# Attention in three sweeps, with each projection as seven products of 2x2 blocks over two token tiles

## The chip, the cores and the metric

One core of one Trainium2 chip runs the whole program. The time is device microseconds of one execution; the number given for a kernel is the median of its runs. The engines are named as the profile names them: PE does matmuls and PE transposes, PEld is its weight load, DVE and ACT are the vector and the scalar engine, POOL is the third one, and SP issues nearly all DMAs here. Everything is float32.

## The reference

The program is one pre-norm transformer block on 2048 tokens of width 1024. Attention runs inside a token: its 32 heads attend to each other, so that scores are a 32 x 32 matrix for each token. The MLP's three matrices (hidden width 2752) are quantized to 16 NF4 codes in blocks of 64 and restored before they are used.

```python
def attn(hidden_states, wq, bq, wk, bk, wv, bv, ...):        # H, D = 32, 32
    q = (hidden_states @ wq.T + bq).reshape(B, S, H, D)
    k = (hidden_states @ wk.T + bk).reshape(B, S, H, D)
    v = (hidden_states @ wv.T + bv).reshape(B, S, H, D)
    scores = jnp.einsum('bshd,bstd->bsht', q, k) / np.sqrt(D)
    probs = jax.nn.softmax(scores, axis=-1)
    return jnp.einsum('bsht,bstd->bshd', probs, v).reshape(B, S, E)

def nf4_quant_dequant(w):                                    # BLOCKSIZE = 64
    flat = w.reshape(-1, BLOCKSIZE)
    absmax = jnp.max(jnp.abs(flat), axis=1, keepdims=True)
    normalized = flat / jnp.where(absmax == 0, 1.0, absmax)
    bounds = (NF4_CODE[:-1] + NF4_CODE[1:]) * 0.5
    return (NF4_CODE[jnp.searchsorted(bounds, normalized)] * absmax).reshape(shape)

def ffn(x, w1, w2, w3):
    gate = jnp.einsum('bsd,hd->bsh', x, nf4_quant_dequant(w1))
    up = jnp.einsum('bsd,hd->bsh', x, nf4_quant_dequant(w2))
    return jnp.einsum('bsh,dh->bsd', jax.nn.silu(gate) * up, nf4_quant_dequant(w3))

x = x + attn(layernorm(x), ...)
x = x + ffn(layernorm(x), w1, w2, w3)
```

## The kernel before

**Attention.** The loop over 16 tiles of 128 tokens (`for i in range(NT)`) keeps all of wq, wk and wv in SBUF (12 MB). A tile is normed (`normed`, DVE and POOL), transposed by PE into `xnT` (and, with its tokens in another order, `xnV`), and projected: `project` at L317 does eight accumulating matmuls of 128 x 128 by 128 x 512 for each half of the output, 48 in all. DVE transposes each half out of PSUM in 32 x 32 blocks (`qk_half` L328, `v_half` L335) and adds the bias. Scores and contexts of the tile before are 32 x 32 matmuls, 128 for each call of `scores` (L345) or `context` (L379), two calls for a tile. Softmax (L359), the residual sum (L398) and the second layer norm are mostly DVE's. `keep_T` (L410) transposes the normed tile for the MLP and stores it, with the four operand differences that the MLP's products need, in DRAM.

**The MLP** works on two halves of 1024 tokens (`tbp`) and on groups of four 128-wide hidden chunks (`GROUPS`: 0 to 3, 4 to 7, ... 20 and 21, the last chunk half wide). A `Unit` (L622) computes gate and up of one chunk for one half, which are a 2x2 block product, by seven products of four matmuls instead of eight. `down` (L697) then multiplies a group's hidden values by its w3 chunks and adds them to the rows in DRAM. The order of the passes is group 0 half 0, group 0 half 1, group 1 half 1, group 1 half 0, and so on. Chunk 0 of half 0 is done plainly (`plain_block`, L557) while the attention of the last tile ends.

**The background.** The generator `background` (L196) restores the MLP's weights, one job of 128 x 1024 values at a time. A job's order is: for each chunk of a group ("1", c) and ("2", c), then ("3", c) for each chunk; 65 jobs in all, twelve for a full group. A job is 15 threshold passes, each an ACT instruction (`sg`, L211) and a DVE instruction (`r`, L214 for the first and L216 for the others), the block maxima and the scaling of the next job's input after the tenth pass (`absmax`, L177; `scaled`, L169: 16 short ACT instructions), and the scaling of its result. Every `yield` of the generator is called a step here: one at the very start and then 17 for each job (16 for the last). `advance(n)` (L228) issues n steps. A finished job is put into `pending`. What is left of it is done by `flush` (L164), which runs the generator `finish` (L134): a first call transposes half of the chunk on PE and copies it, a second does the other half, and a third stores it and enters its key into `wd`. The tile `r` of a job has two buffers, `sg` two, `wn` three and `wop` one.

**What sets the order.** PE's instructions run in the order in which the program writes them (`tc.manual_schedule`, L246). The orders of DVE, ACT and SP are chosen by a planner, from the order of the program, the dependences and the free buffers. Attention calls `advance` with 4, 3, 4, 4 and 3 in each tile. In the MLP `spent` (L534) is called with each product's nominal microseconds (3.43 for a product of four matmuls, 1.7 for each full chunk in each of the eight steps of `down`), issues RATE steps for each of them, and calls `flush(1)` when the running job is past its fifth pass. Whoever needs a restored weight calls `until` (L232) first: `load_w12` (L514) for each unit, `load_w3` (L524) for each chunk of a `down`.

```python
    def until(kind, c):                       # L232
        while (kind, c) not in wd:
            if next(bg, flush) is flush:      # flush is what next returns when bg is at its end
                flush()
```
```python
        if step["n"] in range(5, 15):         # L539, in spent
            flush(1)
        advance(n)
```

Of the kernel before, what the change touches and what calls it, by code (L numbers as in the profile page):

```python
# [12 lines left out]
FP = mybir.dt.float32  # L13
AF = mybir.ActivationFunctionType
ALU = mybir.AluOpType
# [18 lines left out]
RATE = 0.6  # L34
# [17 lines left out]
def preln_block_kernel(  # L52
# [184 lines left out]

    left, right = ExitStack(), ExitStack()
# [3 lines left out]
    ps_pj = left.enter_context(tc.tile_pool(name="ps_pj", bufs=4, space=PSUM, side="left"))  # L242
    work = right.enter_context(tc.tile_pool(name="work", bufs=1, side="right"))
# [4 lines left out]
    hook["pool"] = ps_pj  # L248

    def bank(nm):  # L250
        return hook["pool"].tile([P, TB], FP, tag="pj", name=nm)

    hook["psum"] = lambda half: bank("ptw").rearrange("p (k h) -> p k h", h=P)
    xt = {}

    def load_x(i):
        xt[i] = work.tile([P, E], FP, tag="x", name="xt")
        nc.sync.dma_start(xt[i], xf[ts(i, P), :])

    load_x(0)  # L260
    ws = []
    for nm, w in (("wq", wqT), ("wk", wkT), ("wv", wvT)):
        t = wpool.tile([P, KC, E], FP, tag=nm, name=nm)
        for n in range(2 if nm == "wq" else 1):
            m = 512 if nm == "wq" else E
            for k in range(KC):
                nc.sync.dma_start(t[:, k, ts(n, m)], w[ts(k, P), ts(n, m)])
        ws.append(t)
    biases = []
    for nm, b in (("qb", qb), ("kb", kb), ("vb", vb)):  # L270
        t = wpool.tile([P, 32], FP, tag=nm, name=nm)
        for g in range(4):
            nc.scalar.dma_start(t[g * 32 : (g + 1) * 32, :], b)
        biases.append(t)
    qb_sb, kb_sb, vb_sb = biases
    wq_sb, wk_sb, wv_sb = ws
# [9 lines left out]
    def normed_x(i):  # L286
        return normed(xt.pop(i), work.tile([P, E], FP, tag="xn", name="xn"))

    def transposed(xn, put):

        for half in range(2):
            pt = bank("pt").rearrange("p (k t) -> p k t", t=P)
            for k in range(4):
                nc.tensor.transpose(pt[:, k, :], xn[:, ts(4 * half + k, P)], ident)
            put(half, pt)

    def inputs_T(xn):
        xnT = work.tile([P, KC, P], FP, tag="xnT", name="xnT")

        xnV = work.tile([P, KC, P], FP, tag="xnV", name="xnV")  # L300
        pts = []

        def put(half, pt):
            nc.scalar.copy(xnT[:, ts(half, 4), :], pt)
            pts.append(pt)

        def put_v():
            for half, pt in enumerate(pts):
                nc.scalar.copy(
                    xnV[:, ts(half, 4), :].rearrange("p k (c m) -> p k c m", c=4),  # L310
                    pt.rearrange("p k (m c) -> p k c m", c=4),
                )

        transposed(xn, put)
        return xnT, xnV, put_v

    def project(lhsT, w, n, by_d=False):  # L317

        pj = bank("pj")
        for k in range(KC):  # L320
            rhs, dst = w[:, k, ts(n, 512)], pj
            if by_d:
                rhs = w[:, k, :].rearrange("p (t d) -> p t d", d=D)[:, :, ts(n, 16)]
                dst = pj.rearrange("p (t d) -> p t d", d=16)
            nc.tensor.matmul(dst, lhsT[:, k, :], rhs, start=(k == 0), stop=(k == KC - 1))  # L325
        return pj

    def qk_half(t, pj, n):  # L328

        nc.vector.transpose(  # L330
            t.rearrange("p s h -> p h s")[:, ts(n, 16), :],
            pj.rearrange("p (h d) -> p h d", d=D),
        )

    def v_half(t, pj, n):  # L335

        nc.vector.transpose(
            t.rearrange("p m d -> p d m")[:, ts(n, 16), :],
            pj.rearrange("p (t d) -> p d t", d=16),
        )  # L340

# [16 lines left out]

    def softmax_T(at):  # L359
# [15 lines left out]
        prT = work.tile([P, 32, NH], FP, tag="prT", name="prT")  # L375
# [3 lines left out]
    def context(at, prT, vd, part):  # L379
        for s4 in range(4 * part, 4 * part + 4):  # L380
            for g in range(4):
                m = 8 * g + s4
                for c in range(4):
                    r = slice(c * 32, (c + 1) * 32)
                    nc.tensor.matmul(
                        at[g * 32 : (g + 1) * 32, c, s4 * 32 : (s4 + 1) * 32],
                        prT[r, m, :],
                        vd[r, m, :],
                        start=True,
                        stop=True,  # L390
                    )

    def load_x1(i):
        x1 = work.tile([P, E], FP, tag="x1", name="x1")
        nc.sync.dma_start(x1, xf[ts(i, P), :])
        return x1

    def residual(i, at, x1):  # L398

        cx = work.tile([P, 32, NH], FP, tag="pr", name="cx").rearrange("p a b -> p (a b)")  # L400
# [7 lines left out]

    even = {}

    def keep_T(i, x1n):

        t = work.tile([P, 2, 4, P], FP, tag=f"xT{i % 2}", name="xT")
        transposed(x1n, lambda half, pt: nc.scalar.copy(t[:, half], pt))
# [16 lines left out]

    xnT, xnV, put_v = inputs_T(normed_x(0))
    put_v()
    prev = x1n = None
    for i in range(NT):
        if i + 1 < NT:
            load_x(i + 1)
# [367 lines left out]
```

## Time and profile before

| | us |
|---|---|
| median of 3 runs (2578.46 to 2581.49) | 2580.28 |
| the profiled execution | 2583.84 |
| its span | 2582.1 |
| PE busy in the span | 2503.7 (97%) |
| DVE busy | 1895.3 (73%) |
| ACT busy | 1804.1 (70%) |
| DMA traffic | 402 MB, 156 GB/s |

A group line of the profile names the line of the kernel, the engine and the operation, then output and inputs by tile name with their shapes, and how often it ran; behind the first bar stand its busy time and the mean of one in ns, behind the second the engine's idle time just before such instructions and what ended it. A matmul on 128 x 512 float32 values leaves two records. In a timeline a line is a run of like instructions: start, length, engine, line, operation, and in brackets the idle time before it and its releaser. A table by stage gives busy microseconds of each engine in a stretch of the span, with the number of instructions, the clock granted to PE, the busy share of the DMA engines and their GB/s. Attention lasts until about 843 us, where the first matmul of `plain_block` starts; the first unit begins at about 883, and the twelve calls of `down` start at 966, 1125, 1281, 1440, 1599, 1757, 1914, 2076, 2234, 2391, 2485 and 2546.

### The profile page before, as it was taken

How to read it: one execution, taken by the hardware profiler on the slowest of the kernel's cores; microseconds unless marked ns; L12 is line 12 of the kernel's file. 1: busy time of each engine (PE TensorE's matmuls, PEld its weight loads, DVE VectorE, ACT ScalarE, POOL GpSimd, SP SyncE). 2: the span in 40 equal slices, each digit the busy share in tenths (PEclk: the TensorE clock that was granted, in tenths of full speed). 3: DMA queues.
4: the chain of work that ended last, by engine and by line, in shares of the span. 5: the costliest groups of instructions: out<-in, count | busy, mean ns of one | idle time of the engine just before them, and what ended most of it. 6: DMA issues, size and time to landing. Idle time of an engine off the chain costs nothing.

```text
span 2582.1 us, 36864 instructions
## 1 busy us (share of the span) xinstructions
PE 2503.7 (97%) x14336; PEld 1168.0 (45%) x14336; DVE 1895.3 (73%) x2089; ACT 1804.1 (70%) x3494; POOL 26.5 (1%) x87
## 2 busy tenths in 40 slices
PE   8889999999998899999999999999999999999998
PEld 3445555555554444444444444444444444444433
DVE  4888888888887587787888788777887887751222
ACT  3866565665655597998989898898998998851000
POOL 0000000000000000000000000000000000000000
PEclk9899999999999899999999999999999999999999
DMA  7022222312222866344663346544464354551483
GB/s 261 18 99 97 70 83 91 99 59 91 71 77 89 301 235 235 117 147 175 248 220 142 140 171 248 204 147 155 163 252 171 136 198 160 211 203 66 150 293 138
DMA packets 135167, 402.21 MB, mean 156 GB/s; under 512 B 11664, under 2 KB 65936, under 8 KB 120272
## 3 DMA queue, kind: packets, MB, share of 16 engines
q1 hardware_dynamic: 134416, 399.81, 43.2%
q8 instruction: 112, 1.84, 0.3%
q14 instruction: 63, 0.52, 0.1%
q10 hardware_dynamic: 576, 0.05, 0.0%
HBM read 268.48 MB, written 131.33 MB: 155 GB/s over the span
## 4 chain that ended last, share of the span: by engine, by line
PE 25%; ACT 20%; DVE 17%; issue 6%; DMA 2%; DVEq 0%; SPq 0%; ACTq 0%
DVE r L216 14%; PE po L714 10%; PE z L548 8%; ACT sg L211 8%; ACT r L172 5%; ACT wn L172 4%; PE q L548 3%; PE rr L548 2%; ACT wop L147 1%; DVE am L184 1%; DMA w<-wd 1%; DVE acc L735 1%; PE po L726 1%; PE ptw L146 1%; ACT u L647 0%
## 5 line engine op out<-in xcount | busy, mean ns | idle before, releaser
L211 ACT ACTIVATE sg<-wn,edge 128x1024 f32<-128x1024 f32 (+1 forms) x975 | 1097.6, 1139 | 264.5 <-DVE r L216 241.5
L216 DVE SCALAR_TENSOR_TENSOR r<-sg,r 128x1024 f32<-128x1024 f32 (+1 forms) x910 | 1103.9, 1213 | 122.5 <-ACT sg L211 72.2
L714 PE MATMUL po<-w,h 128*128 128x512 f32 x1344 | 597.5, 599 | 13.8 <-DVE acc L735 10.4
L714 PEld LDWEIGHTS po<-w,h 128*128 128x128 f32 x1344 | 250.7, 191 | 338.8 <-issue 288.6
L548 PE MATMUL z<-xB,w 128*128 128x512 f32 x720 | 322.0, 597 | 2.4 <-DVE h L685 1.4
L548 PE MATMUL z<-xT,w 128*128 128x512 f32 x656 | 297.2, 596 | 3.8 <-ACT g L640 2.9
L548 PE MATMUL q<-xT,w 128*128 128x512 f32 x656 | 291.5, 592 | 0.0
L172 ACT ACTIVATE wn<-wn,rc 128x64 f32<-128x64 f32 x1032 | 267.7, 336 | 26.8 <-DVE rc L192 26.7
L172 ACT ACTIVATE r<-r,am 128x64 f32<-128x64 f32 x1032 | 257.3, 336 | 14.4 <-DVE r L216 14.1
L325 PE MATMUL pj<-wv,xnV 128*128 128x512 f32 x512 | 230.6, 604 | 0.0
L325 PE MATMUL pj<-wq,xnT 128*128 128x512 f32 x512 | 230.1, 603 | 0.0
L325 PE MATMUL pj<-wk,xnT 128*128 128x512 f32 x512 | 227.9, 598 | 0.0
L735 DVE TENSOR_TENSOR acc<-acc,po 128x512 f32<-128x512 f32 x192 | 129.9, 682 | 132.8 <-PE po L714 87.3
L548 PEld LDWEIGHTS z<-xB,w 128*128 128x128 f32 x720 | 135.7, 192 | 167.6 <-issue 158.5
L548 PEld LDWEIGHTS z<-xT,w 128*128 128x128 f32 x656 | 122.9, 191 | 152.5 <-issue 139.3
L548 PEld LDWEIGHTS q<-xT,w 128*128 128x128 f32 x656 | 123.1, 190 | 148.1 <-issue 145.2
L184 DVE TENSOR_REDUCE am<-wn 128x16 f32<-128x1024 f32 (+1 forms) x65 | 78.6, 1209 | 144.7 <-ACT r L172 142.6
L147 ACT COPY wop<-ptw 128x512 f32<-128x512 f32 (+1 forms) x130 | 74.4, 573 | 128.4 <-PE ptw L146 128.4
L325 PEld LDWEIGHTS pj<-wv,xnV 128*128 128x128 f32 x512 | 97.5, 193 | 118.0 <-issue 117.1
L548 PE MATMUL rr<-xB,w 128*128 128x512 f32 x328 | 147.5, 592 | 0.0
L325 PEld LDWEIGHTS pj<-wq,xnT 128*128 128x128 f32 x512 | 96.4, 193 | 111.3 <-issue 107.0
L325 PEld LDWEIGHTS pj<-wk,xnT 128*128 128x128 f32 x512 | 94.8, 190 | 109.3 <-issue 108.1
(74 smaller groups left out, 1396.9 us busy)
## 6 DMA issues: line engine op xcount, KB each, us to landing
w<-wd SPq DMA_DIRECT2D x41, 1280.0 KB, 6.9
acc<-x1d SPq DMA_DIRECT2D x96, 512.0 KB, 3.9
wd<-wop SPq DMA_DIRECT2D x21, 2048.0 KB, 7.2
w<-wd SPq DMA_DIRECT2D x83, 512.0 KB, 4.8
x1d<-acc SPq DMA_DIRECT2D x80, 512.0 KB, 2.9
wn<-in_w_dram SPq DMA_DIRECT2D x63, 512.0 KB, 3.8
xT<-xdT SPq DMA_DIRECT2D x28, 1024.0 KB, 7.5
xB<-xdB SPq DMA_DIRECT2D x24, 1024.0 KB, 6.4
```

Source lines behind the costliest of these rows:

```text
L146: nc.tensor.transpose(pt[:q, k, :], v[:, j * q : (j + 1) * q], ident)
L147: nc.scalar.copy(o[:q, first + half], pt[:q])
L172: nc.scalar.mul(dst[:, ts(n, BLOCK)], src[:, ts(n, BLOCK)], by[:, n : n + 1])
L184: nc.vector.tensor_reduce(am[:, :nb], v.rearrange("p (b e) -> p b e", e=BLOCK), AX.X, ALU.max, apply_absolute_value=True,)
L211: nc.scalar.activation(t, v, AF.Identity, bias=edge[:, i : i + 1], scale=BIG)
L216: nc.vector.scalar_tensor_tensor(r, t, code, r, ALU.min, ALU.max)
L325: nc.tensor.matmul(dst, lhsT[:, k, :], rhs, start=(k == 0), stop=(k == KC - 1))
L548: nc.tensor.matmul(dst, w[:, k, :], xop[:, k, :], start=start and k == 0, stop=stop and k == 3, skip_group_check=True,)
L714: nc.tensor.matmul(po, hs[c][j][:, ts(q, P)], w3T[c][:, ts(n, 512)], start=(c == g[0]), stop=(c == g[-1]), skip_group_check=True,)
L726: nc.tensor.matmul(po, hs[NFULL][r, ts(q, P)], w3T[NFULL][r, ts(n, 512)], start=False, stop=True, skip_group_check=True,)
L735: nc.vector.tensor_tensor(a[:, ts(n, 512)], a[:, ts(n, 512)], po, ALU.add)
```

## The change

The loop over tiles becomes three sweeps over eight pairs of tiles. The first does all queries, the second all keys with scores and softmax, the third all values with contexts, residual sums and the MLP's operands. Between sweeps, queries (`qD`), probabilities (`pD`) and the projections' input operands (`opD`, and `opV` with the tokens in the other order) are kept in DRAM.

In a sweep, a pair of tiles is the two rows of a 2x2 block product: the 1024 inputs are cut into two halves, and the 1024 outputs too. `products` does it by seven products of four matmuls, as the MLP's units do. For that four differences of the transposed input are made on DVE (`differences`, once for each order of the tokens), four of each weight (T1 to T4; those of wk and wv are made piece by piece in the first sweep, by `weight_chunk`, and stored in `wtD`), ACT copies four partial sums and one result out of PSUM, and DVE adds three. Only one matrix's seven 1 MB operands are in SBUF at a time; in the last pair of a sweep each is replaced by that of the next matrix after its last product. The 32 x 32 block transposes on DVE now read a whole row of 1024 from SBUF instead of halves from PSUM.

`advance` is called with 1, 1, 1 and 2 in a pair of the first sweep, with 1, 2, 2 and 2 in the second, and with 2, 2, 2 and 3 in the third. RATE goes from 0.6 to 0.62. `until`, `spent`, `flush`, the units and `down` are as they were.

```diff
-RATE = 0.6
+RATE = 0.62
...
-    def project(lhsT, w, n, by_d=False):
-
-        pj = bank("pj")
-        for k in range(KC):
...
+    def products(A, fill1, fill2, used=lambda name: None):
...
+        z = ps_pj.tile([P, TB], FP, tag="z", name="z")
+        mul(z, SA11, "B11", True, False)
+        g0 = copied("g0", z)
+        q = ps_pj.tile([P, TB], FP, tag="q", name="q")
+        mul(q, S3, "T3", True, False)
+        s7 = copied("s7", q)
+        fill1()
+        mul(z, S2, "T2", False, False)
+        u2 = copied("u2", z)
+        r = bank("r")
+        mul(r, SA12, "B21", True, True)
+        ce = pair.tile([P, E], FP, tag="C0", name="ce")
+        co = pair.tile([P, E], FP, tag="C1", name="co")
+        nc.vector.tensor_tensor(ce[:, 0:512], g0, r, ALU.add)
+        mul(z, S1, "T1", False, False)
+        u4 = copied("u4", z)
+        nc.vector.tensor_tensor(co[:, 512:], u4, s7, ALU.add)
+        fill2()
+        mul(z, S4, "B22", False, True)
+        nc.scalar.copy(ce[:, 512:], z)
+        mul(q, SA22, "T4", False, True)
+        nc.vector.tensor_tensor(co[:, 0:512], u2, q, ALU.add)
+        return ce, co
+
+    def differences(t):
+
+        nc.vector.tensor_tensor(t[:, S1], t[:, SA21], t[:, SA22], ALU.add)
+        nc.vector.tensor_tensor(t[:, S2], t[:, S1], t[:, SA11], ALU.subtract)
+        nc.vector.tensor_tensor(t[:, S3], t[:, SA11], t[:, SA21], ALU.subtract)
+        nc.vector.tensor_tensor(t[:, S4], t[:, SA12], t[:, S2], ALU.subtract)
...
+    for p in range(NP):
+        more = p + 1 < NP
+        now = nxt
+        if more:
+            load_x(2 * p + 2)
+            load_x(2 * p + 3)
+            nxt = Inputs(p + 1)
+        advance(1)
+
+        def fill1():
+            if more:
+                nxt.transposes(0)
+            flush(1)
+            advance(1)
+
+        def fill2():
+            if more:
+                nxt.transposes(1)
+            flush(1)
+            advance(1)
+
+        cs = products(now.A, fill1, fill2, (lambda name: None) if more else next_W("k"))
+        flush(1)
+        if more:
+            nxt.finished()
+        for j in range(2):
+            t = work.tile([P, 32, NH], FP, tag="qd", name="qd", bufs=2)
+            qk_T(t, cs[j], qb_sb)
+            nc.sync.dma_start(qD[2 * p + j], t)
+        if more:
+            nxt.finished_v()
+        weight_chunk("kv"[p // 4], p % 4)
+        advance(2)
...
+    for p in range(NP):
+        nextA = load_A(opD, p + 1) if p + 1 < NP else load_A(opV, 0)
+        qd = load_tiles(qD, p, "ql", 4)
+        advance(1)
+
+        def fill1():
+            if prev is not None:
+                attend(2 * p - 2, prev[0][0], prev[1][0])
+            advance(2)
+
+        def fill2():
+            flush(1)
+            if prev is not None:
+                attend(2 * p - 1, prev[0][1], prev[1][1])
+            advance(2)
...
+            qk_T(t, cs[j], kb_sb)
+            kd.append(t)
+        advance(2)
...
-    for i in range(NT):
...
-        advance(4)
...
-        advance(3)
...
-        advance(4)
...
-        advance(4)
...
-        advance(3)
-        prev = (qd, kd, vd)
+    for p in range(NP):
+        nextA = load_A(opV, p + 1) if p + 1 < NP else None
...
+        advance(2)
+
+        def fill1():
+            if i - 1 in x1n:
+                keep_T(i - 1, x1n.pop(i - 1))
+            if prev is None:
+                attend(NT - 2, kept[0][0], kept[1][0])
+            else:
+                x1n[i] = gather(i, prev[0][0], prev[1][0], x1s[0])
+            advance(2)
+
+        def fill2():
+            flush(1)
+            if prev is None:
+                attend(NT - 1, kept[0][1], kept[1][1])
+            else:
+                x1n[i + 1] = gather(i + 1, prev[0][1], prev[1][1], x1s[1])
+            advance(2)
+
+        cs = products(A, fill1, fill2)
+        flush(1)
...
+            v_T(t, cs[j], vb_sb)
+            vd.append(t)
+        advance(3)
+        A, prev = nextA, (load_tiles(pD, p, "pl", 3), vd)
```

## The prediction

> **What bounds the kernel now.** I read the table by stage first, then the groups, then the order of PE and the pace of the dequantization.
>
> ```profile
> 8.00:842.00 834.00, 798.57 (x9769) 405.87 (x9772) 694.62 (x744) 506.26 (x973) 22.74 (x60) 0.98 0.28 93
> 842.00:1281.00 439.00, 427.91 (x1415) 195.81 (x1406) 333.92 (x365) 365.21 (x697) 1.73 (x2) 0.98 0.56 204
> 1281.00:1840.00 559.00, 554.45 (x1397) 248.56 (x1396) 446.20 (x493) 503.39 (x992) 0.00 (x0) 1.00 0.50 182
> 1840.00:2582.00 742.00, 722.76 (x1783) 317.71 (x1781) 418.24 (x485) 429.19 (x835) 0.00 (x0) 0.99 0.49 178
> ```
>
> Columns: stretch, its us, busy us of PE, PEld, DVE, ACT, POOL, granted clock, DMA share, GB/s. Attention is the first row, the rest is the MLP. PE is the bound in both; ACT is second in the MLP (503 of 559), DVE in attention (695 of 834). PE does one tile each 49.7 us, (776.01 - 328.73) / 9, by these two starts in the timeline, and in the chain 24 records take 10.30 us: 0.429 us a record, 0.858 a matmul (two records), 3.43 a product of four.
>
> ```profile
> 328.73 7.13 PE L325 MATMUL pj<-wq,xnT 128*128 128x512 f32 x16
> 776.01 7.13 PE L325 MATMUL pj<-wq,xnT 128*128 128x512 f32 x16
> ```
> ```profile
> 1061.55 10.30 PE z L548 x24
> ```
>
> PE keeps its written order. In this timeline it stood 14.68 us before four transposes of a dequantized chunk, until ACT had scaled it, although the next projection was independent of them:
>
> ```profile
> 53.61 7.03 PE L325 MATMUL pj<-wq,xnT 128*128 128x512 f32 x16
> 75.32 1.91 PE L146 MATMUL ptw<-ident,r 128*128 128x128 f32 x4 [14.68 <-ACT r L172]
> 77.02 9.16 PE L325 MATMUL pj<-wq,xnT 128*128 128x512 f32 x16
> ```
>
> Dequantization at its densest: a job is 15 threshold passes, and begins on DVE with line 214. Three whole jobs lie between the first and last of these starts, 27.7 us each; in that stretch ACT was busy 80.27 of 83.30 us.
>
> ```profile
> 1325.03 0.69 DVE L214 TENSOR_SCALAR r<-sg 128x1024 f32<-128x1024 f32 x1
> 1352.21 0.69 DVE L214 TENSOR_SCALAR r<-sg 128x1024 f32<-128x1024 f32 x1
> 1408.26 0.69 DVE L214 TENSOR_SCALAR r<-sg 128x1024 f32<-128x1024 f32 x1
> ```
> ```profile
> 1325.00:1408.30 83.30, 82.53 (x209) 36.89 (x208) 68.38 (x76) 80.27 (x160) 0.00 (x0) 1.00 0.49 173
> ```
>
> The prices, from the groups:
>
> ```profile
> L330 DVE STREAM_TRANSPOSE qd<-pj 128x512 f32<-128x512 f32 x32 | 33.2, 1062 | 26.2 <-PE pj L325 26.2
> L376 DVE STREAM_TRANSPOSE prT<-pr 128x1024 f32<-128x1024 f32 x16 | 19.6, 1224 | 0.0
> L650 DVE TENSOR_TENSOR g<-g,rr 128x512 f32<-128x512 f32 x41 | 28.0, 682 | 67.6 <-PE rr L548 67.6
> L647 ACT COPY u<-z 128x512 f32<-128x512 f32 x41 | 23.3, 569 | 122.3 <-PE z L548 122.3
> L146 PE MATMUL ptw<-ident,r 128*128 128x128 f32 (+1 forms) x520 | 79.2, 274 | 14.9 <-ACT r L172 14.7 <-ACT wop L147 0.2
> ```
>
> **Part 1: the products.** Two tiles took 96 matmuls, now 3 x 28 = 84: 12 x 0.858 = 10.3 us less. Layer-norm transposes, scores and contexts stay. Background steps per pair fall from 36 to 5 + 7 + 9 = 21; a job is 17 steps and eight transposes of 0.152 us (79.2 / 520), so 15 / 17 x 8 x 0.152 = 1.1 less. PE per pair: 99.4 - 11.4 = 88.0, eight pairs 704.
>
> DVE per pair, by means. Before: 12 half transposes 12.8, six biases 7.3, two norms 4.7, two residuals 11.1, four operand differences 2.7, two softmaxes 12.8, 36 steps at 1.19 (20.2 a job / 17) 42.8: 94.2, where the windows show 87 per 99.4 (records overlap; factor 0.92). After: 9 sums at 0.682 = 6.1, 8 input differences 5.5, 4 weight differences 2.7, 21 steps 25.0, and six whole transposes from SBUF. These the trace does not show: 1.22 is the plain one (L376), 2 x 1.06 the permuted half (L330); I take 2.0, since the write pattern stays L330's: 12.0. With the unchanged 38.6 that is 89.9, x 0.92 = 82.8, or 94% of PE's 88.0 (78 to 83.5). PE stays the bound; now at 94% instead of 87%, DVE costs it 10 us by my estimate, between 0 and 60 (DVE running at 88% only). ACT adds 15 copies of 0.57 a pair, 8.6, and loses 15 steps of 1.54 (a job's 16.9 + 8.1 + 1.1 = 26.1, / 17), 23: no cost.
>
> Start: the old loop spent 843 - 16 x 49.7 = 48 us on start and end waits. Now two tiles are normed, transposed and subtracted, and three 2048-wide weight differences (2.4 each, twice 1.22) run before T2, but 4 MB of weights suffice instead of 12. I leave 48, between 30 and 70. Attention: 704 + 48 + 10 = 762, against 843: -81.
>
> Queues: about 30 more DMAs a pair on SP at 0.3 to 0.5 us of issue, some 12 us of 88, and 115 MB more in 762 us, about 150 GB/s on top of 93; slice 1 of the page moved 261. The stores of inputs, q and probabilities are read a sweep later, and weights are replaced one by one behind their last product, 3.43 us or more ahead of use. Worst DMA wait of DVE here: 3.9 us in two. I take 0, at worst 3 us a pair, inside the 60 above. The tail (plain block, two contexts, three operand stores) goes from 41 to 44.
>
> **Part 2: the background's lead.** This decides. A job is 17 steps after one first step; job ("3",7), the 24th, is whole at step 409. Attention used to give 16 x 18 = 288 steps, now 8 x 21 = 168; the tail 5, now 4. Up to the third call of down (group 4 to 7, half 1), which needs ("3",7), spent was called for eleven units (24.0 each), two downs and one product: 72.0 + 54.4 + 96.0 + 54.4 + 96.0 + 3.4 = 376.3 us. Before: 293 + 0.6 x 376.3 = 518 steps. Trace: by 1281.0, where this down begins, lines 214 and 216 ran 17 + 14 and 238 + 190 times, 459; 518 steps are 30 jobs and 7 passes, 457. The count holds. After: 172 + 0.62 x 376.3 = 405, four short. And later it is shorter still: a group of four needs 12 x 17 = 204 steps, its 301.0 us give 187.
>
> until then does not make up four steps. It advances while wd lacks the key, but wd is only filled by flush, and until calls flush only when the background is exhausted. So all 700 remaining steps are issued there, with 41 jobs unflushed. Afterwards spent flushes a third of a job at each call: PE meets the transposes of job after job in its written order, three calls apart (10.3 us in products, 20.6 in down), and each waits for that job, which costs ACT 26 us; behind the waiting transposes lie the next products, and behind those the units' evictions on ACT and DVE. r has two buffers, so ACT can't run ahead. PE waits for ACT through 41 jobs.
>
> Pace: 80.27 / 3 = 26.8 of ACT a job, with 2.2 units' copies (about 1.8 us a job); here a job has half as many: 25.9 if ACT never idles. Low 24.8 (line 214 from 903.29 to 928.13). High 30: passes alternating with DVE started 1.33 apart in attention (301.45, 302.78), x 15 = 20.0, plus scaling 8.1, copies 1.1 and the units' 0.9. I take 26.5, near the dense stretch: 40.5 jobs (the last is half wide) x 26.5 = 1073 (1004 to 1215), and 12 us until ("3",7) itself is through store and load (2.8 + 4.8 us and four steps). The 123 spent calls of these 41 jobs are the PE work from 1281 to about 1840: 559. So +526. Behind it 742 us less 16 jobs' transposes (20): 722, -20. Up to there the MLP keeps its 398 us (883 to 1281); RATE 0.62 asks a job per 27.4 us, about what the dense stretch gave.
>
> PE pauses some 13 us a job. After the 14.68 us pause, 16 records took 9.16 us instead of 7.03, 2.1 more; 41 pauses are 87 us of PE, all within PE's 514 us of waiting: 0.
>
> The Trainium skill (TensorE: Matmul & The Clock Gate, "HAM oscillation") speaks against such a loop: an idle window of about 3.4 us halves the clock until PE was busy for one. By it a pause would cost 1.7 us, an estimate from that page, 70 in all; on the path it would make 3078 of my 3008, but the row above prices the same effect and PE has room for it.
>
> Sum against the profiled execution, 2583.8 (span 2582.1): -81 + 3 + 526 - 20 = 3012; that execution is 3.6 above the median, so 3008.
>
> **The rivals.**
> - *No exhaustion* (faster). If the lead sufficed, -81 + 3 and up to 15 for a fuller ACT: 2502 to 2517. It decides if 409 steps and their flushes are there at the third down and 613 at the fifth; my count gives that only from a RATE of about 0.68. Against it: 457 counted, 459 seen.
> - *Exhaustion, but PE is not held*: a planner may set the transposes elsewhere. Then PE loses only what ACT lacks: about 2520 to 2750. The 14.68 us wait speaks against it.
> - *The slow pace*: ACT's queue, with DVE's, stands at the units' copies too, 30 us a job: +142, and attention bound by DVE, +50: 3150 to 3200.
> - *The products save nothing*: no; 672 matmuls for 768 are written, and PE was 99.6% busy there.
>
> **How the numbers follow.** Mine (2900 to 3130) 0.74; slow pace 0.14; not held 0.06, nearly all slower; no exhaustion 0.06. Within 0.2%, about what tells apart here, 0.01. Range 2870 to 3180: from 1004 us of jobs and a good start (-69 - 30, and some slack) to 30 us a job with part of the DVE loss.
>
> **What would show it.** Right: first MLP matmul near 765; pj-like products 12 fewer a pair; from about 1200 to 2290 ACT over 90% busy, PE about half, PE's longest waits at line 146's transposes on ACT's scaling; then over 700 us with ACT nearly idle. Wrong: no such stretch, which would mean that until flushes or the steps were enough; or jobs much farther apart than 27 us, with ACT waiting for PE.

## The result and the profile after

The changed kernel takes 3224.25 us (median, 3221.23 to 3225.41) against 2579.37 for the old one beside it: 1.25 times as long, 95% interval 1.2478 to 1.2522. The prediction was 3008 us, 2870 to 3180. The profiled execution of the changed kernel has a span of 3223.6 us, 641.5 more than the old one's 2582.1.

The table by stage of the changed kernel (stretch, its length, busy us of PE, PEld, DVE, ACT and POOL, granted clock, DMA share, GB/s): attention, the MLP up to the third down, the stretch that the prediction called the run-out of the background, and the rest.

```profile
8.00:941.00 933.00, 762.28 (x9328) 383.46 (x9329) 688.26 (x750) 417.57 (x795) 33.86 (x59) 0.90 0.55 196
941.00:1403.00 462.00, 438.04 (x1592) 200.63 (x1592) 323.92 (x356) 352.44 (x677) 1.82 (x4) 0.97 0.54 196
1403.00:2506.50 1103.50, 699.40 (x1579) 306.41 (x1580) 870.51 (x917) 1037.27 (x2057) 0.00 (x0) 0.80 0.33 119
2506.50:3223.00 716.50, 701.35 (x1646) 304.04 (x1645) 127.02 (x186) 52.45 (x88) 0.00 (x0) 0.99 0.43 155
```

The third row is as foreseen: ACT is busy for 94% of 1103.5 us and PE for 63%; in the fourth ACT is nearly idle and PE is the bound again. The first row is not: attention takes 933 us from 8 to 941, where 834 stood before, and PE's clock is 0.90 there instead of 0.98.

The waits of PE, longest first (us in all, times, longest):

```profile
PE ptw L146 <- ACT r L172: 248.9, 27, 12.9
PE ptw L146 <- ACT wop L147: 62.9, 12, 14.8
PE pt L430 <- ACT AV L433: 58.4, 17, 8.9
PE sc L380 <- issue: 44.4, 16, 5.6
PE cx L394 <- issue: 43.2, 14, 4.5
PE z L305 <- ACT u L832: 30.2, 4, 10.2
PE po L899 <- DVE h L847: 30.2, 4, 9.1
```

The first two are the run-out, and so is nearly all of the last two (29.9 and 27.4 us of them fall into its stretch). In the timeline of PE, these transposes of four dequantized chunks stand behind waits of 12 us, and the distance from one to the next is a job:

```profile
1859.25 1.90 PE L146 MATMUL ptw<-ident,r 128*128 128x128 f32 x4 [12.51 <-ACT r L172]
1886.53 1.90 PE L146 MATMUL ptw<-ident,r 128*128 128x128 f32 x4 [12.69 <-ACT r L172]
...
1939.36 1.91 PE L146 MATMUL ptw<-ident,r 128*128 128x128 f32 x4 [11.56 <-ACT r L172]
1965.33 1.91 PE L146 MATMUL ptw<-ident,r 128*128 128x128 f32 x4 [12.17 <-ACT r L172]
```

1939.36 to 1965.33 is 26.0 us, 1859.25 to 1939.36 three jobs of 26.7; the whole stretch is 1103.5 / 41 = 26.9 a job. 26.5 was predicted.

The three rows between are new; they belong to attention, and of the third 8.9 us to the tail. For them the counting has to be clear: a small float32 matmul leaves two records as well, so a call of `scores` or `context` is 64 matmuls and leaves 128 records. The 128 for each call in the description of the old kernel, and the counts of small matmuls in the expectations, are counts of records, and so are all counts from here on.

In the second sweep, a tile's two calls of `scores`, 256 records, are issued in one go. PE starts, stops in the middle with nothing to wait for that the profile shows, and the products behind run slower:

```profile
562.25 2.01 PE L380 MATMUL sc<-kd,ql 32*32 32x32 f32 x214
569.86 0.70 PE L380 MATMUL sc<-kd,ql 32*32 32x32 f32 x42 [5.60 <-issue]
570.49 5.78 PE L305 MATMUL z<-wT,A 128*128 128x512 f32 x8
576.11 3.60 PE L305 MATMUL r<-wB,A 128*128 128x512 f32 x8
```

Eight records took 5.78 us right after the gap and 3.60 a product later; the granted clock was 0.50 from 567.9 to 574.7 us and 1.00 from 576.2 to 579.7. The first sweep has a wait of another kind: the transposes of a tile's second half stand until ACT has copied the first half in the other token order, and ACT has background work in between.

```profile
105.81 0.60 PE L430 MATMUL pt<-ident,xn 128*128 128x128 f32 x4
115.30 1.11 PE L430 MATMUL pt<-ident,xn 128*128 128x128 f32 x4 [8.89 <-ACT AV L433]
116.21 5.85 PE L305 MATMUL z<-wT,A 128*128 128x512 f32 x8
```

By stretches of the two spans the account is as follows. The borders are the first matmul of the plain block (843.0 and 941.0), the first unit (883.4 and 993.8), the third down (1281 and 1403) and the end of the transposes of the last job, or what answers to it (1840 and 2506.5).

| | before | after | difference | predicted |
|---|---|---|---|---|
| attention | 843.0 | 941.0 | +98.0 | -81 |
| tail | 40.4 | 52.8 | +12.4 | +3 |
| MLP to the third down | 397.6 | 409.2 | +11.6 | 0 |
| run-out | 559.0 | 1103.5 | +544.5 | +526 |
| rest | 742.1 | 717.1 | -25.0 | -20 |
| sum | 2582.1 | 3223.6 | +641.5 | +428 |

The miss of 213 us is a miss of 179 in attention, 21 in the two rows after it and 18 in the run-out, less 5.

PE's own time splits the 179. The prediction took 11.4 us of work off each pair, 91 in all; by the first rows of the two tables by stage PE was busy 36 us less (798.57 to 762.28). So some 55 us are work that ran slower, and the other 124 are waiting, beyond the 10 that were counted for DVE.

### The profile page after: what moved, and what is told of

Read it like the earlier page. It is cut to its first block, busy times and chain, and to the rows that moved or that the text cites. A ratio compares the mean times of both kernels' runs of the same rounds, so it can differ in the third digit from the quotient of the medians.

```text
span 3223.6 us, 37123 instructions
## 1 busy us (share of the span) xinstructions
PE 2601.1 (81%) x14144; PEld 1194.5 (37%) x14144; DVE 2012.6 (62%) x2213; ACT 1859.7 (58%) x3614; POOL 37.3 (1%) x87
## 3 DMA queue, kind: packets, MB, share of 16 engines
q1 hardware_dynamic: 159280, 515.16, 44.4%
## 4 chain that ended last, share of the span: by engine, by line
PE 31%; ACT 21%; DVE 14%; issue 4%; DMA 2%; DVEq 0%; SPq 0%; ACTq 0%
DVE r L216 13%; PE z L305 12%; ACT sg L211 11%; PE po L899 10%; ACT wn L172 5%; PE q L305 4%; ACT r L172 4%; PE rr L305 3%; PE ptw L146 2%; ACT wop L147 1%; DMA out_dram<-acc 1%; DMA wd<-wop 0%; PE po L911 0%; DMA w<-wd 0%; DMA xB<-xdB 0%
## 5 line engine op out<-in xcount | busy, mean ns | idle before, releaser
L899 PE MATMUL po<-w,h 128*128 128x512 f32 x1344 | 615.6, 615 | 58.1 <-DVE h L847 30.2
L305 PE MATMUL z<-xB,w 128*128 128x512 f32 x720 | 351.1, 640 | 35.1 <-ACT u L839 22.0
L146 PE MATMUL ptw<-ident,r 128*128 128x128 f32 (+1 forms) x520 | 118.0, 323 | 313.9 <-ACT r L172 248.9
L305 PE MATMUL z<-xT,w 128*128 128x512 f32 x656 | 312.9, 622 | 30.2 <-ACT u L832 30.2
L832 ACT COPY u<-z 128x512 f32<-128x512 f32 x41 | 23.5, 574 | 414.6 <-PE z L305 414.6
L146 PEld LDWEIGHTS ptw<-ident,r 128*128 128x128 f32 (+1 forms) x520 | 72.1, 152 | 418.6 <-ACT r L172 301.6
L305 PE MATMUL z<-wT,A 128*128 128x512 f32 x384 | 206.0, 686 | 1.8 <-ACT u L323 1.3
L305 PE MATMUL z<-wB,A 128*128 128x512 f32 x384 | 200.2, 670 | 2.3 <-ACT u L323 2.3
L305 PE MATMUL q<-wT,A 128*128 128x512 f32 x384 | 172.6, 592 | 0.0
L184 DVE TENSOR_REDUCE am<-wn 128x16 f32<-128x1024 f32 (+1 forms) x65 | 78.4, 1207 | 144.5 <-ACT r L172 144.4
L835 DVE TENSOR_TENSOR g<-g,rr 128x512 f32<-128x512 f32 x41 | 28.0, 684 | 159.8 <-PE rr L305 159.8
```

The lines of the kernel that those rows point to most:

```text
L146: nc.tensor.transpose(pt[:q, k, :], v[:, j * q : (j + 1) * q], ident)
L184: nc.vector.tensor_reduce(am[:, :nb], v.rearrange("p (b e) -> p b e", e=BLOCK), AX.X, ALU.max, apply_absolute_value=True,)
L305: nc.tensor.matmul(dst, w[:, k, :], xop[:, k, :], start=start and k == 0, stop=stop and k == 3, skip_group_check=True,)
L832: nc.scalar.copy(u2, self.z)
L835: nc.vector.tensor_tensor(self.g0, self.g0, r, ALU.add)
L899: nc.tensor.matmul(po, hs[c][j][:, ts(q, P)], w3T[c][:, ts(n, 512)], start=(c == g[0]), stop=(c == g[-1]), skip_group_check=True,)
```

## The experiments

Times, and two marks of each profiled execution: the first product of the plain block, where attention ends, and what lies between the first `rr` product of the first unit and the end of the span, called MLP here. The rest of the tail lies between the two.

| kernel | us | ratio to before, 95% interval | attention ends | MLP |
|---|---|---|---|---|
| before | 2579.37 | | 843.0 | 1683 |
| after | 3224.25 | 1.2478 to 1.2522 | 941.0 | 2220 |
| e1: until flushes | 2824.89 | 1.0930 to 1.0967 | 940.7 | 1819 |
| e2: RATE 0.70 | 2810.21 | 1.0878 to 1.0911 | 939.2 | 1807 |
| e3: before, RATE 0.50 | 2800.49 | 1.0831 to 1.0874 | 842.9 | 1903 |
| e4: before, calls adjacent | 2680.43 | 1.0367 to 1.0402 | 941.6 | 1683 |
| e5: e1, calls split | 2756.36 | 1.0671 to 1.0711 | 877.2 | 1813 |
| e6: e5, four PSUM tiles | 2705.28 | 1.0472 to 1.0508 | 830.1 | 1815 |
| e7: e1, scaling on DVE | 2790.36 | 1.0804 to 1.0853 | 931.9 | 1793 |
| e9: e6 and e7, RATE 0.68 | 2603.10 | 1.0077 to 1.0107 | 835.2 | 1717 |
| e10: e9, less on DVE | 2616.77 | 1.0126 to 1.0160 | 848.6 | 1718 |
| e11: e10, RATE 0.66 | 2642.14 | 1.0220 to 1.0251 | 847.8 | 1745 |
| e12: e9, other product order | 2599.20 | 1.0060 to 1.0088 | 823.5 | 1714 |

In e10 and e11 the tail's first contexts, 256 records, stand ahead of the plain block, so that this mark comes later there by that work. The profiled execution of e12 is its fastest, 2588.86 us where the median is 2599.20, so that its marks are some 10 us better than usual.

**Is the run-out what costs the MLP its time?** Three kernels. The first lets `until` flush at every step:

```diff
         while (kind, c) not in wd:
-            if next(bg, flush) is flush:
-                flush()
+            flush()
+            next(bg, None)
```

> The changed kernel, with one edit in until: it flushes before each step that it issues, so that it makes up only the steps that are missing (by the count 5, 18, 17 and 18 at four calls of down) and does not run the background out. Theory (the run-out makes PE meet 41 jobs at ACT's pace, 1085 us where PE had 559 us of work): about 500 us go, 2730 us, between 2690 and 2800; no stretch is left in which PE waits at line 146 for most jobs. Rival (ACT is simply short by the 120 steps that attention no longer does, and PE would wait for it in any case): the time stays above 3000. Both: the stretch before the first unit, 989 us, does not change.

The second leaves `until` as it is and gives the background a larger lead: `RATE = 0.70` instead of 0.62.

> The changed kernel with RATE 0.70 instead of 0.62, nothing else. By the count no call of until then finds its key missing, so the background is never run out. Theory: 2740 us, between 2690 and 2850 (933 steps in the MLP cost ACT some 1430 to 1530 us, and PE waits a little for them). Rival (the background is too slow whatever its order): above 3000.

The third brings the run-out into the old kernel, with nothing else of the change: `RATE = 0.5` instead of 0.6.

> The kernel before, with its attention untouched and RATE 0.50 instead of 0.60. By the count until then runs the background out at the seventh call of down, for job (3,13), with 19 jobs behind it. Theory: those cost 18.5 x 26.5 = 490 us and 12 us of start, in place of some 240 us of PE work: 2842 us, between 2790 and 2890. Rival (the loss in the changed kernel belongs to the new attention, its buffers and its traffic, not to until): a rate lower by a sixth leaves 2580 to 2620.

Measured: 399 and 414 us less than the changed kernel by the one and by the other edit, and 220 us more in the old kernel, whose table by stage (e3, columns as above) then has such a stretch too (PE 62% busy, ACT 91%):

```profile
1900.00:2400.00 500.00, 309.50 (x728) 138.29 (x729) 383.52 (x407) 456.12 (x901) 0.00 (x0) 0.81 0.33 118
```

The mechanism holds: four missing steps and an `until` that does not flush. e2 and e3 lie in the ranges expected for them. But e1 did not come down to the 2690 to 2800 that was expected. Its attention is untouched, and its MLP is still 136 us longer than the old one (1819 against 1683). What is left there, by these rows of the list of PE's waits of e1 (us in all, times, longest):

```profile
PE ptw L146 <- ACT r L172: 65.5, 4, 20.4
...
PE po L899 <- DMA w<-wd: 22.8, 5, 8.5
PE ptw L146 <- ACT wop L147: 19.5, 9, 4.1
```

The lead is still too short, so that a few downs wait for their newest chunk through scaling, transposes, store and load. With RATE 0.70 most of this goes (17.9 us before the transposes are left, and no wait for `w`), and other waits come: the units' copies on ACT, 28.9 and 27.7 us, behind a background that keeps ACT 93% busy (464.43 of 500 us from 1900 on).

**Is it ACT's time that is short?** The 16 small ACT instructions that scale a job's input become one multiplication on DVE, on top of e1 (written in short here):

```diff
-            scaled(v, v, rc, nb)                       # 16 x ACT, 128 x 64 each
+            nc.vector.tensor_tensor(v as [P, nb, 64], same, rc broadcast over 64, ALU.mult)
```

> On top of the kernel with the flush in until (2825 us), the calls unsplit: the scaling of a job's input, 16 small instructions of ACT, becomes one multiplication on DVE. Theory (with the flush in until, what is left of the loss in the MLP is a lack of ACT time, 26 us a job at 89 to 93% busy): ACT needs about 22 us a job, the MLP falls from about 1830 to 1700 to 1750, the whole to 2700 to 2750, and ACT's share there to some 80%. Rival (what is left is the order, PE's waits for particular chunks, or DVE, which gets 1.2 us more a job): within 25 us of 2825, or slower.

Measured 34.5 us less, not 75 to 125, and a little more than the 25 of the rival. ACT did fall, from 91% in e1 (456.65 of the same 500 us) to 81% in this row of the table by stage of e7. But PE rose only from 93% (466.97) to 95%, and waited for the same chunks (43.8, 21.3 and 19.5 us in three lines like those above):

```profile
1900.00:2400.00 500.00, 473.46 (x1194) 214.08 (x1192) 424.50 (x460) 402.98 (x627) 0.00 (x0) 0.98 0.49 177
```

My reading of these waits is that with RATE 0.62 the lead is short, and with RATE 0.70 ACT is. Only both edits together take most of the loss away: in the kernel with everything mended (below) the MLP is 1717 us, 102 less than in e1. The scaling alone gave 26 of e1's MLP, and RATE 0.70, without the flush, comes out 12 below e1.

**Do 256 records of small matmuls in one go cost attention its time?** In the old kernel, each first call (128 records) is moved next to the second one; nothing else changes:

```diff
-            scores(at, prev[0], prev[1], 0)
+            pass
 ...
+            scores(at, prev[0], prev[1], 0)
             scores(at, prev[0], prev[1], 1)
 ...
-            context(cx, prT, prev[2], 0)
+            pass
 ...
+            context(cx, prT, prev[2], 0)
             context(cx, prT, prev[2], 1)
```

> The kernel before, with the two calls of scores of a tile put next to each other, and the two of context, as the changed kernel has them: 256 matmuls of 32 x 32 in one go instead of twice 128. Theory (PE runs out of instructions inside such a run: one block of 128 matmuls with their weight loads is used up in 1.2 us, faster than the next arrives): a gap put down to issue in nearly each of the 30 calls, 1.5 to 3 us long at this kernel's DMA traffic, with the products behind it at a lower clock: 2640 to 2700 us. Rival (the gaps in the changed kernel come from its heavier DMA traffic or from its PSUM tiles): no gaps, 2575 to 2590.

Measured 100.5 us more, all of it in attention (843.0 to 941.6; the MLP takes 1683 in both). By the rows of the table by stage PE is also busy for longer in e4's attention, 827.82 us at a clock of 0.93 where 798.57 at 0.98 stood, so that the slower products behind the gaps cost some 29 us here. Two rows of PE's waits in e4, and one gap in its timeline:

```profile
PE sc L351 <- issue: 50.7, 13, 6.2
PE cx L385 <- issue: 35.0, 13, 5.2
```
```profile
434.64 2.09 PE L351 MATMUL sc<-kd,qd 32*32 32x32 f32 x224
440.16 0.42 PE L351 MATMUL sc<-kd,qd 32*32 32x32 f32 x32 [3.43 <-issue]
440.51 9.52 PE L325 MATMUL pj<-wk,xnT 128*128 128x512 f32 x16
```

Where the gap falls is telling. In the ten score calls of this kernel from 148 to 671 us the parts before it have 186, 194, 201, 209, 216, 224, 231, 239, 246 and 254 records: 7.5 more each tile. A tile is 96 records of products, 512 of small matmuls, 16 transposes of inputs and 8.5 of the background (18 steps; a job of 17 has eight), 632.5 in all, 7.5 short of five times 128. The cut stays at each 128th matmul record of PE's program, and of the two cuts in a pair of calls it is the second one that starves.

The reverse, in the changed kernel with e1's edit: each run of 256 records becomes two of 128, with a product of four between.

```diff
-        scores(at, qd, kd, 0)
-        scores(at, qd, kd, 1)
+        scores(at, qd, kd, 0)          # in fill1 and fill2, as before
 ...
         u2 = copied("u2", z)
+        mid1()                         # scores(..., 1) or context(..., 1) of the open tile
         r = bank("r")
 ...
         nc.scalar.copy(ce[:, 512:], z)
+        mid2()                         # the same
```

> On top of the kernel with the flush in until (2825 us): each call of 256 small matmuls of scores or contexts in the sweeps is split into two of 128, with a product of four (3.43 us) between the halves; nothing is added or left out. Theory (256 in one go outrun the supply of instructions): the gaps put down to issue, 45.4 + 43.6 us there, fall below 25 in all, the products behind them come back from 5 to 6.6 us to 3.5 to 4, and the time falls by 110 to 150: 2675 to 2715. The clock in the second and third sweep rises to 0.95 or more. Rival (the gaps come from the 115 MB of additional transfers, which stand before instruction fetches wherever the calls lie): the number of gaps stays near 27, and the time within 30 of 2825.

Measured 68.5 us less, 63 of it in attention. The gaps go (`sc` from 45.4 to 5.0 us, `cx` to 12.3, of which most is in the unsplit tail), with the same transfers as before, so the rival falls. But the gain is half of what was expected. Some 73 us of gaps left attention, and the work behind them became faster too: PE is busy 12.1 us less in the second sweep (259.55 to 247.49, at a clock of 0.98 instead of 0.91) and 5.5 less in the third (236.97 to 231.52, at 0.92 instead of 0.89, not the 0.95 expected). Yet only 63 came back, because other waits grew by nearly 30 us, those for running sums on ACT and for second layer norms on DVE above all (`z` on `u` from 3.8 to 11.6, `pt` on `x` from 2.2 to 9.7). The second sweep gave 44 us (309.7 to 265.3, from the first score to the first context matmul), the third 19.

Where the cuts come from, the traces show in the row of the instruction queue among the DMA queues (packets, MB, share of the engines), first of the old kernel and then of the changed one:

```profile
q8 instruction: 112, 1.84, 0.3%
q8 instruction: 111, 1.82, 0.2%
```

That is 16.4 KB a packet. The old kernel's trace has 14336 matmul records with a weight load each, the changed one's 14144; in packets of 256 instructions these are 112 and 110.5. The times of the packets tie them to the gaps. In the gap of the changed kernel shown above, which begins at 564.26, a packet of q8 moves from 567.46 to 568.43, and PE goes on at 569.86. In all 32 gaps that the changed kernel has before "issue", and in all 28 of e4, PE goes on 1.2 to 1.6 us after a packet of q8 has landed, while in attention such a packet comes only every 12 us. Numbering PE's matmul records through, the remainder of the gaps' numbers by 128 falls slowly and in order, from 91 to 69 in the changed kernel and from 91 to 82 in e4. So PE waits there for its next block of instructions. Why a block comes too late is open; e4's gaps are as long in sum as the changed kernel's, at less than half the DMA traffic in attention (84 against 196 GB/s).

The Trainium skill (Runtime: NRT & Kernel Launch, "Instruction fetch mechanics") says that instructions come in 16 KiB blocks of 256, which agrees with both counts, and that the cost is mostly hidden, which the runs here do not bear out: 87.6 us of gaps in the changed kernel (44.4 and 43.2), up to 5.6 us each.

**The first sweep.** Four PSUM tiles of one bank instead of one tile of four, and the copies in the other token order set behind the product of B22, on top of e5 (the PSUM tile of scores and contexts is then opened after this sweep):

```diff
-            self.at = ps_at.tile([P, 4, 4, P], FP, tag="at", name="pt")
+            self.at = [ps_t.tile([P, 4, P], FP, tag=f"t{n}", name="pt") for n in range(4)]
 ...
-                nc.scalar.copy(self.V[:, n] ..., pt ...)      # in transposes
+        def other_order(self): ...                             # the four copies, called in mid2
```

> The split calls, and in the first sweep four PSUM tiles of one bank for the transposes in place of one tile of four, with the copies in the other token order set behind the product of B22. Theory (the one tile and the single buffer behind it hold PE in the first sweep): PE's wait for the copies of line 433, 58 us in 17 waits, goes, and with it the slow products behind: 60 to 80 us less than the split calls alone, 2600 to 2650. The first sweep's pair goes from 36 to about 28 us. Rival (the first sweep is bound by DVE, with weight differences, norms and six kinds of input differences there): the wait turns up at other DVE work, and less than 25 us is gained.

Measured 51.1 us less, below the 60 to 80 expected; the first sweep ends 46.7 us earlier (340.3 to 293.6 by the first score matmul). The wait on the copies of AV is gone from PE's list. Which of the two edits did it was not tried.

**All together**, with the tail's contexts split too, the scaling on DVE, and RATE 0.68:

```diff
-RATE = 0.62
+RATE = 0.68
```

> All together: flush in until, calls split in the sweeps and in the tail, four PSUM tiles, input scaling on DVE, RATE 0.68. If the three causes (run-out 399 with the flush, calls about 130, first sweep about 70) add and the ACT lack goes with the scaling on DVE (about 100), 3224 - 399 - 130 - 70 - 100 = 2525; 2490 to 2580, which would be faster than the old kernel (2579) by up to 3%. If the lead is still short, 2580 to 2650.

Measured 2603.10, above the 2490 to 2580 of the sum, in the 2580 to 2650 said for a lead still too short, and 0.9% above the old kernel. 621 us of the changed kernel's 645 are accounted for by the chain: 399 by the flush, 69 by the split calls, 51 by the first sweep, 102 by lead, scaling and the tail's split together. But no time is left over for what seven products were to save: attention ends at 835 against 843, and the MLP is 34 us longer than the old one. Of these 34, 18 are transposes of the background, which moved out of attention with their steps (448 records and 76.3 us behind the first `rr` product, for 390 and 58.4 before), and most of the rest is waiting.

**What holds attention then?** The predicted 762 us are missed by 73 even here. Two attempts. In the first, DVE gets 43 us less by the rows (layer-norm scaling and input differences in the other order go to ACT), and the tail's first contexts stand ahead of the plain block:

```diff
-        nc.vector.tensor_scalar(dst, src, mv[:, 0:1], rs, ALU.subtract, ALU.mult)
+        nc.scalar.activation(dst, src, AF.Identity, bias=nm, scale=rs)      # nm = -mean * rs, on DVE
 ...
-            differences(self.V)
+            for n in range(7): nc.scalar.copy(self.V[:, n] ..., self.A[:, n] ...)
```

> On top of the kernel with everything mended (2603 us): in the first sweep the inputs in the other token order are copied by ACT from the finished ones (7 copies a pair instead of 4 copies and 4 differences on DVE), the scaling of a layer norm goes from DVE to ACT (one activation of 1024 columns a tile), and in the tail the first contexts stand ahead of the plain block's first product. Theory (what is still missing of the predicted 762 us of attention is DVE, 90 to 95% busy in the first sweep and over 85% in the third): DVE loses 4 x 0.6 + 2 x 0.75 = 3.9 us a pair in the first sweep and 1.5 in the third, 43 in all, and most of it comes back: the plain block begins near 800 instead of 835, the time is 2560 to 2580. Rival (the order of the waits at the start, the operand loads and the lower clock hold it, not DVE): the plain block begins at 825 or later, 2590 to 2605. Which side of 2579 it ends is open.

> The last kernel at RATE 0.66 instead of 0.68. By the count of steps three advances of until are then forced, of 1, 1 and 4 steps. If the dense background holds units back (PE waits of 1 to 3 us on ACT's copies), 5 to 15 us less than at 0.68; if the lead matters more, the three forced places cost 5 to 20 us each: 15 to 50 more. Within 5 us: neither.

Measured 13.7 us more. DVE fell to 79% in the first sweep (214.53 of 272 us, from 242.94), but the last product of the sweeps ends only 1.2 us earlier (818.1 to 816.9). The rest of the tail, from there to the first `rr` product, takes 78.4 us instead of 68.7, and there the tail's new order was changed together with the norms; which of the two cost it was not tried. In the sweeps DVE is busy 39 us less in all (689.16 to 650.03), and PE now waits for ACT in DVE's place, by the list of PE's waits of e10:

```profile
PE z L315 <- ACT u L333: 30.8, 15, 3.8
PE pt L445 <- ACT xn L310: 18.9, 2, 10.4
PE pt L669 <- ACT x L310: 15.3, 5, 6.5
```

DVE's total was not the limit. And e11, with `RATE = 0.66`, costs 25.4 us more than e10, as was said for a lead that matters more.

In the second attempt, on top of the kernel with everything mended, the last two products change places:

```diff
-        mul(z, S4, "B22", False, True)
-        nc.scalar.copy(ce[:, 512:], z)
-        mid2()
         mul(q, SA22, "T4", False, True)
         nc.vector.tensor_tensor(co[:, 0:512], u2, q, ALU.add)
+        mid2()
+        mul(z, S4, "B22", False, True)
+        nc.scalar.copy(ce[:, 512:], z)
```

and the loads of the plain block's weights and first operands are written ahead of the residual inputs.

> On top of the kernel with everything mended (2603 us; norms and copies of the first sweep as there): the last two products of a set change places, so that ACT's copy of the running sum u4 has a product of 3.43 us more before that sum goes on; and at the start of the tail the plain block's weights and first two operands are loaded ahead of the residual inputs. Theory (what is left of attention's shortfall are single waits of 1 to 3 us at the running sum, with products of over 5 us behind them): of the 13.5 us of waits on line 331 most goes, with 8 to 12 us of slow products, and the load wait of 16.2 us falls to 5 to 10: 2570 to 2590, the plain block beginning at 810 to 820. Rival (DVE or the loads set the pace, and a removed wait turns up at the next input): the plain block begins at 830 or later and the time is 2595 to 2610.

Measured 2599.20, which is 4 us less, within what tells two such kernels apart. The waits at the running sum did not go, they moved to the next set's first product, which follows at once on the same bank (29.4 us, where 13.5 stood at the running sum); and the operand load, which still follows the last set, is awaited no less than before (18.0 us for 16.2; the list of PE's waits of e12):

```profile
PE z L313 <- ACT ce L357: 29.4, 19, 5.5
PE z L313 <- DMA xB<-xdB: 18.0, 1, 18.0
```

My reading, which no run shows, is that four products in one PSUM bank, each followed by a copy, need four other products to cover the copies, and the set has three. What a third order would give was not tried. No version of the change was found that beats the old kernel.

## Why the prediction was too low

**What bounds the kernel, and the background's lead: right.** The run-out begins at the third down, ends with the last job, and runs at ACT's pace, 26.9 us a job for 26.5 said. Its term was +526 and is +544.5. The rest, -20 said, is -25. The rival "no exhaustion" is excluded by the trace, and so is "PE is not held": PE stood 311.8 us before these transposes alone. The slow pace, 30 us a job, falls with the 26.9.

**The step that failed is in part 1: "Layer-norm transposes, scores and contexts stay."** Their work stays, 41.7 us for the 4096 score records of the old kernel, but their order does not, and a moved step was costed at nothing. The term -81 was mis-sized by 179 us. By the runs, 64 of these are the calls put together to 256 records in one go (e5; in the old kernel, without any other part of the change, the same step costs 99 us, e4), and 47 the transposes that were gathered in one PSUM tile with the copies behind them (e6). The remaining 68 of e6 (830.1 against 762) are not settled: 15.0 of them are the wait for the plain block's operands, which the prediction had not thought of; among the others are single waits for running sums, norms and loads, which came back elsewhere when they were removed (e10, e12), and work at a lower clock (0.94 from 17 to 289 us of e6).

The row that prices the first of these was in the profile of before. In the tail of the old attention, where no product stands between the two context calls of the last tile, the old kernel's timeline has

```profile
859.21 1.70 PE L385 MATMUL cx<-vd,prT 32*32 32x32 f32 x179
866.65 1.05 PE L385 MATMUL cx<-vd,prT 32*32 32x32 f32 x77 [5.73 <-issue]
```

In the loop, the two calls of a tile stood apart, with products between. By this row, an estimate, 32 pairs of calls put together would have cost up to 32 x 5.73 = 183 us; the gaps that came were 78.7 in attention (44.4 and 34.3) and 8.9 in the tail. A range from 0 to 183 for that step would have held its price, and attention's +98 too, though the latter by luck, since the transposes have a part in it. I read the diff's `attend` and `gather` as the same calls in another place.

**DVE: the size was right, the bound was not.** The whole transposes were taken at 2.0 us and are 1.98, by this row of the changed kernel's groups:

```profile
L366 DVE STREAM_TRANSPOSE vd<-ce 128x1024 f32<-128x1024 f32 x8 | 15.8, 1979 | 3.7 <-ACT ce L345 3.7
```

But the 0 to 60 us for a slower attention were hung on DVE alone, and in e10 39 us less of DVE's work let the sweeps end only 1.2 us earlier. Waits of ACT's copies in PE's written order were considered for the MLP and not for the sweeps. The clock, set at no cost by the 14.68 us row, was covered in the run-out, as said. In attention, where PE is the bound, it was not looked at, and there it cost: 0.90 instead of 0.98, with some 55 us of PE's work that ran slower.

**The rivals' prices.** "No exhaustion" was priced at 2502 to 2517. With the lead in place (e2) the kernel takes 2810, and with everything mended 2603: it would have been slower than before too. The condition, a RATE of about 0.68, fits what was tried (no run-out at 0.70 without the flush, and 25.4 us more at 0.66 than at 0.68 with it); that ACT at 93% busy then delays the units (56.6 us of waits) was taken for "up to 15 for a fuller ACT". The 60 more transposes that the MLP then gets were left out of this price. So the chance of .06 for a faster kernel stood for a case that none of these runs shows.

## What to carry to other kernels

Before a step is costed as moved and unchanged, look at what stood between its parts: small instructions that were spread among long ones may not be issued back to back at the same pace, and one gap in the old trace, even in a corner that costs nothing, prices it. A generator that runs ahead and a consumer that forces it should be counted step by step at each place where it is forced; here four missing steps of 409 cost 400 us, and a slower RATE brings the same loss into the old kernel. And mending a lead may use up the time of the engine that does the work ahead: here a higher RATE came out 12 us better, a lighter ACT 26, and both together 102.

## What the runs showed of the hardware

Dense 32 x 32 matmuls on PE can stop at the cuts after each 128th matmul record of the program, until the next packet of instructions has landed. In runs of 256 records, 30 of 32 had such a gap, 0.9 to 5.6 us, at the second cut in the run; with a product of 3.43 us after each 128, 17.3 us in all are left of 89.0 (e5 against e1).

A pause need not be long to slow what follows: in this timeline of e10, a wait of 2.28 us behind 1.04 us of transposes is followed by eight records in 5.40 us, where 3.60 is the rule. The granted clock was 0.50 from 137.6 to 140.9 us and 1.00 in the 3.3 us before. The Trainium skill (TensorE: Matmul & The Clock Gate, "HAM oscillation") speaks of idle stretches above some 3.4 us; here 2.28 us without any work of PE, 3.3 without a product, were enough.

```profile
133.66 1.04 PE L445 MATMUL pt<-ident,xn 128*128 128x128 f32 x8
136.97 5.40 PE L315 MATMUL z<-wB,A 128*128 128x512 f32 x8 [2.28 <-ACT u L333]
142.20 3.60 PE L315 MATMUL q<-wT,A 128*128 128x512 f32 x8
```
